# Two layers of cross-attention on one core: feature blocks loaded in quarters, a row load moved in the queue, and three changes of order

## The chip, the core and the metric

The kernel runs on one core of a Trainium2 chip. The core has TensorE (PE in the profile; its weight loads are a row of their own, PEld), VectorE (DVE), ScalarE (ACT), GpSimd (POOL) and SyncE (SP), which here only issues transfers. Sixteen DMA engines carry all transfers. The metric is the device time of one execution in microseconds (us); lower is better.

## The reference

Eight batches of 100 query rows (`x`, 8x100x1024) attend to 1444 context rows of width 512 (`ctx_512`), twice, in fp32. Cut to what is computed:

```python
# layer 0
Q = x @ Wq + bq;  K = ctx @ Wk + bk;  V = ctx @ Wv + bv
w = softmax(Q @ K.T * 1024**-0.5, axis=-1)          # over the 1444 keys
x = x + (w @ V) @ Wo + bo
# layer 1, with its own weights
q = x @ Wq + bq;  k = ctx @ Wk + bk;  v = ctx @ Wv + bv
w = softmax(q @ k.T * 1024**-0.5, axis=1)            # over the 100 queries
y = w @ v + x
out = (y - mean(y)) * rsqrt(var(y) + 1e-6) * gamma + beta
```

## The kernel before

**Algebra.** Keys and values are never made. The kernel multiplies the weights first (`qk` is Wq times Wk transposed, `vo` is Wv times Wo), turns the queries of all batches into `g` (512 rows, 100 columns for each batch), and gets the scores of a batch as context features times `g`. The weighted context `A` (512 x 100) is context rows times softmax weights, and only `A` meets `vo` (layer 0) or Wv (layer 1). So every batch and layer reads the context twice: transposed, as four feature blocks `cT_b_0` to `cT_b_3` of 128 x 1444, and plain, as four row tiles `c_b_0` to `c_b_3` of three 128 x 512 blocks each. Large products go through a seven-product scheme with sums made on VectorE; these are the names `qk_x`, `g_y`, `o_z_x` and so on.

**Stages of the profiled execution.** `qk` of layer 0 to 54 us, `vo` to 100.5, queries of layer 0 to 137, `qk` of layer 1 to 184, then layer 0's scores and weighted rows to 333, its projection to 362, queries of layer 1 to 393, layer 1's scores and weighted rows (with two projections between) to 580, the last batch's projection and normalisation to the end.

**Scores and weighted rows.** `scores_by_keys` (line 941) runs over the four feature blocks k and in each over the twelve key blocks m in the order `KEYS` (8, 11, 9, 10, 0 to 7). `weighted_rows` (902) runs over m = 0 to 11 and four column blocks. From batch 0 on, `alternated` (1317) weaves one step of `A` of batch b with one step of the scores of batch b + 2. TensorE's program order is written out by hand; the order of the other engines is set by a scheduler at build time, except for instructions marked to stay in program order. `vector.in_order` (95) marks VectorE's.

**Loads.** All context loads are issued from SP in program order through `loaded_in_order` (859). In the instruction list each SP transfer waits for one of eight DMA semaphores in turn, which is that of the transfer eight before it, and for the release of its buffer. `load_features` (862) loads each block in two parts, columns 0 to 703 and 704 to 1443. `load_rows` (871) loads a batch's rows in 13 transfers. Buffers go in rotation: row tiles and the first two feature blocks of a batch use the ten buffers of `unit` (74), which the weight products use too; blocks 2 and 3 use the three buffers of `feature_block` (86). So `cT_1_3` takes the buffer of `cT_0_2`, and can be loaded only when the scores of batch 0 have used that. `loaded` (1305) takes blocks from several loads in turn.

**Start of layer 0.** `first_scores` loads four blocks and runs a batch's scores. Lines 1329 to 1332 do batch 0, then batch 1, and `alternated(0)` then loads `c_0` and `cT_2` in turn. SP's order is therefore `cT_0`, `cT_1`, then `c_0_0`, `cT_2_0`, `c_0_1`, `cT_2_1` and so on.

**Softmax.** The key blocks are split in groups `ROWS`: 8 to 10, 0 to 3, 4 to 7, and block 11 (`REST`) by itself. `softmax0` (981) takes maxima, makes the exponents' argument from PSUM and takes the exponent, group by group in that order. `softmax1` (1125) moves the scores out of PSUM with the bias, then for each group finds the maximum over queries and takes exponents, then divides each group (`rtotal`); the order is 8 to 10, 11, 0 to 3, 4 to 7. Both end with `weight_sums` (1159), which adds the blocks on POOL.

**Other places touched.** After the weighted rows of batch 6, the two first parts of `project0` (1041) run: four half products into `o_x` and `o_z`, and an inner seven-product `o_z_*`, each added to `xT` on VectorE by `add_to_queries` (1021). In batch 7, at steps 7, 11 and 15, `queries` (657) is advanced, which issues the sums S1, S2 (`g_s`) and S3 (`qk<-qk`) of layer 1's queries on VectorE; they are not marked in order. In the projection of batches 4 to 6, `project1` (1193) advances batch 7's softmax by 1, 1, 1, 1 and 2 steps in the first five of seven products, and by the rest after the last.

Of the kernel before, what the change touches and what calls it, by code (L numbers as in the profile page):

```python
# [34 lines left out]
S, L = 1444, 512  # L35
EC, LC = E // P, L // P
NQ = 4
MC = 12
# [8 lines left out]
REST = range(11, 12)  # L47
KEYS = (8, 11, 9, 10, *range(8))
LAST = (MC - 1) * P
# [6 lines left out]
def two_layer_cross_attention(ctx: ExitStack, tc: tile.TileContext, a: dict, out: bass.AP):  # L56
# [29 lines left out]
    def feature_block(name):  # L86
        return work.tile([P, S], F32, tag="prob", name=name, bufs=3)
# [16 lines left out]
    vector = Vector()  # L104
# [38 lines left out]
    def run(*parts):  # L143

        parts = list(parts)
        while parts:
            parts = [g for g in parts if next(g, parts) is not parts]
# [714 lines left out]
    def load_features(b):  # L862

        for k in range(LC):
            name = f"cT_{b}_{k}"
            t = feature_block(name) if k >= LC // 2 else unit(name)[:, :S]
            for part in (slice(0, LAST // 2), slice(LAST // 2, S)):
                loaded_in_order(t[:, part], a["ctxT"][b][k * P : (k + 1) * P, part])
            yield t

    def load_rows(b):

        src = a["ctx_512"][b]
        for q in range(NQ):
            t = unit(f"c_{b}_{q}").rearrange("p (c l) -> p c l", c=CQ)
            n = CQ - (q == NQ - 1)
            r0 = q * CQ * P
            for i in range(n):
                loaded_in_order(t[:, i, :], src[r0 + i * P : r0 + (i + 1) * P, :])
            if n < CQ:  # L880
                more = PAD - (S - LAST)
                loaded_in_order(t[: S - LAST, n, :], src[LAST:S, :])
                loaded_in_order(t[S - LAST : PAD, n, :], src[:more, :])
            yield t

    def keys(m):

        return P if m < MC - 1 else S - LAST
# [92 lines left out]
    def softmax0(s, groups, rest):  # L981

        b, w = s["b"], s["w"]
        n = keys(MC - 1)
        last = w[:n, MC - 1, :]
        most = work.tile([P, len(groups), T], F32, tag="most", name=f"most_{b}", bufs=1)
        for g, (ms, r, ps) in enumerate(groups):
            ordered, vector.in_order = vector.in_order, vector.in_order or g == 0
            vector.tensor_reduce(most[:, g, :], ps.rearrange("p c t -> p t c"), AX.X, ALU.max)
            if g == 0:  # L990
                vector.tensor_copy(last, rest[0])
                vector.in_order = ordered
                vector.tensor_tensor(last, rest[1], last, ALU.add)
                vector.tensor_tensor(most[:n, g, :], most[:n, g, :], last, ALU.max)
        groups = [*groups, (REST, n, last.unsqueeze(1))]
        vector.tensor_reduce(top[:, :T], most.rearrange("p g t -> p t g"), AX.X, ALU.max)
        nb = P // QD
        turned = work.tile([QD, nb, nb, QD], F32, tag="turned", name=f"turned_{b}", bufs=1)
        for q in range(nb):
            vector.transpose(turned[:, :, q, :], top[q * QD : (q + 1) * QD, :].rearrange("p (n j) -> p n j", j=QD))  # L1000
        best = small.tile([QD, nb], F32, tag="best", name=f"best_{b}")
        vector.tensor_reduce(best, turned.rearrange("p n q j -> p n (q j)"), AX.X, ALU.max)
        spread = turned[:, :, 0, :]
        vector.tensor_copy(spread, best.unsqueeze(2).to_broadcast([QD, nb, QD]))
        shift = work.tile([P, P], F32, tag="shift", name=f"shift_{b}", bufs=1)
        for q in range(nb):
            vector.transpose(shift[q * QD : (q + 1) * QD, :].rearrange("p (n j) -> p n j", j=QD), spread)
        bias, shift = kb0[:, b * T : (b + 1) * T], shift[:, :T]
        vector.scalar_tensor_tensor(shift, shift, SCALE, bias, ALU.mult, ALU.add)
        vector.tensor_tensor(shift, bias, shift, ALU.subtract)  # L1010
        for ms, r, ps in groups:
            n = len(ms)
            rows = w[:r, ms[0] : ms[0] + n, :]
            vector.scalar_tensor_tensor(
                rows, ps, SCALE, shift[:r].unsqueeze(1).to_broadcast([r, n, T]), ALU.mult, ALU.add
            )
            nc.scalar.activation(rows, rows, AF.Exp)  # L1017
            yield
        weight_sums(s)
# [105 lines left out]
    def softmax1(s, scores, rest):  # L1125

        b, w = s["b"], s["w"]
        groups = []
        for ms, r, ps in [scores[0], (REST, keys(MC - 1), rest[0].unsqueeze(1)), *scores[1:]]:
            n = len(ms)  # L1130
            rows = w[:r, ms[0] : ms[0] + n, :]
            bias = kb1[:r, b * T : (b + 1) * T].unsqueeze(1).to_broadcast([r, n, T])
            ordered, vector.in_order = vector.in_order, vector.in_order or len(groups) < 2
            vector.scalar_tensor_tensor(rows, ps, SCALE, bias, ALU.mult, ALU.add)
            vector.in_order = ordered
            if r < P:
                vector.scalar_tensor_tensor(rows[:, 0, :], rest[1], SCALE, rows[:, 0, :], ALU.mult, ALU.add)
            groups.append((ms, r, rows))
            yield
        made = []  # L1140
        for g, (ms, r, rows) in enumerate(groups):
            negmax, total, rtotal = (
                small.tile([P, GM], F32, tag=n, name=f"{n}_{b}_{g}", bufs=4)[:r, : len(ms)]
                for n in ("negmax1", "total1", "rtotal1")
            )
            vector.tensor_reduce(negmax, rows, AX.X, ALU.max, negate=True)
            for i in range(len(ms)):
                nc.scalar.activation(  # L1148
                    rows[:, i, :], rows[:, i, :], AF.Exp, bias=negmax[:, i : i + 1], accum_out=total[:, i : i + 1]
                )  # L1150
            made.append((rows, total, rtotal))
            yield
        for rows, total, rtotal in made:
            vector.reciprocal(rtotal, total)
            vector.tensor_tensor(rows, rows, rtotal.unsqueeze(2).to_broadcast(list(rows.shape)), ALU.mult)
            yield
        weight_sums(s)
# [144 lines left out]
    batches = [{"b": b} for b in range(B)]  # L1302
    A0 = [wide(f"A0T_{g}") for g in range(2)]

    def loaded(*loads):

        got = [[] for _ in loads]
        for _ in range(NQ):
            for load, to in zip(loads, got):
                to.append(next(load))  # L1310
        return got

    def first_scores(b, layer, softmax):

        return scores_by_keys(batches[b], layer, *loaded(load_features(b)), softmax)

    def alternated(b, layer, softmax, dst, first=0):

        nxt = b + 2 < B
        c, *cT = loaded(load_rows(b), *([load_features(b + 2)] if nxt else []))  # L1320
        A = weighted_rows(batches[b], layer, c, dst)
        ahead = scores_by_keys(batches[b + 2], layer, *cT, softmax) if nxt else iter(())
        run(islice(ahead, first))
        for _ in range(MC * LC):
            next(A)
            next(ahead, None)
            yield

    run(first_scores(0, 0, softmax0))
    block_sums("u1", acc_u, sums[:, :LC, :], late=True)  # L1330
    block_sums("wqbk1", acc_c, sums[:, LC : LC + EC, :], late=True)
    run(first_scores(1, 0, softmax0))
    for b in range(B):
        dst = A0[b // G][:, :, b % G * T : (b % G + 1) * T]
        steps = alternated(b, 0, softmax0, dst, 0 if b else MC)
        if b == B - 2:
            o0 = project0(AS, A0)
            parts = [next(o0), next(o0)]
        if b < B - 1:
            run(steps)  # L1340
        if b == B - 2:
            for part in parts:
                run(part)
        if b == B - 1:
            gT[1], queries1 = queries(1, wqk1, u1)
            for n, _ in enumerate(steps):
                if n in (7, 11, 15):
                    next(queries1)
        for e in range(2 * b, 2 * b + 2) if 2 * b < EC else ():
            add_out_bias(e)  # L1350
        if b == 1:
            got = totals("k1", sums[:, : LC + EC, :], LC + EC)
            u1, wqbk1 = got[:, :LC], got[:, LC:]
            vector.in_order = True
            AS = value_sums(wvo)
            vector.in_order = False
# [5 lines left out]
    steps = queries1  # L1362
# [28 lines left out]
    for bs in SETS:  # L1391
# [10 lines left out]
        if b == B - 2:  # L1402
            first = last_columns(wv1)
# [32 lines left out]
```

## Time and profile before

| What | Value |
|---|---|
| Runs shown | 597.15, 594.76, 597.09 us; median 597.09 |
| The profiled execution's own time | 597.27 us |
| Its span | 595.5 us |
| VectorE, ScalarE, GpSimd busy | 397.5, 134.8, 133.8 us |
| Scores and weighted rows together, share of the chain that ended last | A 21%, s 20% |
| Transfers `c<-in_ctx` of 256 KB | 176, median 6.0 us to landing |
| Transfers `cT<-in_ctxT` of 352 and 370 KB | 64 and 64, median 5.9 and 6.4 us to landing |
| Queue 8, instructions | 59 packets, 0.97 MB |

The span runs from the first to the last of the program's own instructions; the profiled execution's time is 1.77 us longer. Busy shares are averages over stages with different limits, so each step of the prediction is read in its own stretch. In a line of waits the three numbers are the total, the number of waits and the longest; "issue" is a wait for nothing that the profile shows.

### The profile page before, as it was taken

How to read it: one execution, taken by the hardware profiler on the slowest of the kernel's cores; microseconds unless marked ns; L12 is line 12 of the kernel's file. 1: busy time of each engine (PE TensorE's matmuls, PEld its weight loads, DVE VectorE, ACT ScalarE, POOL GpSimd, SP SyncE). 2: the span in 40 equal slices, each digit the busy share in tenths (PEclk: the TensorE clock that was granted, in tenths of full speed). 3: DMA queues.
4: the chain of work that ended last, by engine and by line, in shares of the span. 5: the costliest groups of instructions: out<-in, count | busy, mean ns of one | idle time of the engine just before them, and what ended most of it. 6: DMA issues, size and time to landing. Idle time of an engine off the chain costs nothing.

```text
span 595.5 us, 17451 instructions
## 1 busy us (share of the span) xinstructions
PE 576.7 (97%) x7470; PEld 498.1 (84%) x7470; DVE 397.5 (67%) x936; ACT 134.8 (23%) x349; POOL 133.8 (22%) x206
## 2 busy tenths in 40 slices
PE   9999999999999999999998999999999999999994
PEld 8887457678899899999996766787999999999982
DVE  1997589879676973856648587867433347754795
ACT  1321311423510112222001000203333302153313
POOL 3110110221211222331024001205722202341052
PEclk9999999999999999999999999999999999999998
DMA  8959989943696999999981707709999990699114
GB/s 273 308 107 318 303 217 297 255 86 87 119 277 161 387 378 373 373 342 374 366 290 52 248 0 261 230 21 359 363 372 343 359 341 23 181 324 285 37 30 83
DMA packets 65096, 142.95 MB, mean 240 GB/s; under 512 B 7548, under 2 KB 12924, under 8 KB 65020
## 3 DMA queue, kind: packets, MB, share of 16 engines
q1 hardware_dynamic: 56574, 117.80, 56.5%
q0 software_dynamic: 8048, 23.57, 18.9%
q8 instruction: 59, 0.97, 0.7%
q10 hardware_dynamic: 398, 0.47, 0.3%
q14 instruction: 17, 0.14, 0.1%
HBM read 121.53 MB, written 6.14 MB: 214 GB/s over the span
## 4 chain that ended last, share of the span: by engine, by line
PE 92%; issue 3%; DMA 2%; POOL 2%; DVE 1%; ACT 1%; DVEq 0%; POOLq 0%; SPq 0%
PE A L910 21%; PE s L957 20%; PE qk_x L166 7%; PE g_x L166 5%; PE o_x L166 5%; PE vo_x L166 3%; PE o_y L166 3%; PE g_y L166 3%; PE qk_z L166 2%; PE qk_y L166 2%; DMA cT<-in_ctxT 1%; PE o_w L166 1%; PE o_z L166 1%; PE qk_w L166 1%; PE vo_y L166 1%
## 5 line engine op out<-in xcount | busy, mean ns | idle before, releaser
L910 PE MATMUL A<-w,c 128*64 128x100 f32 (+1 forms) x3072 | 229.2, 249 | 3.9 <-issue 2.4
L910 PEld LDWEIGHTS A<-w,c 128*64 128x64 f32 (+1 forms) x3072 | 200.5, 137 | 6.7 <-issue 6.5
L957 PE MATMUL s<-g1T,cT 128*64 128x100 f32 (+1 forms) x1472 | 114.7, 249 | 1.4 <-issue 1.4
L957 PE MATMUL s<-g0T,cT 128*64 128x100 f32 (+1 forms) x1472 | 112.6, 249 | 3.0 <-issue 1.6
L957 PEld LDWEIGHTS s<-g1T,cT 128*64 128x64 f32 (+1 forms) x1472 | 99.0, 136 | 3.5 <-issue 2.8
L957 PEld LDWEIGHTS s<-g0T,cT 128*64 128x64 f32 (+1 forms) x1472 | 97.5, 136 | 4.9 <-issue 2.6
L1168 POOL TENSOR_TENSOR part<-w 128x500 f32<-128x500 f32 x16 | 23.4, 1462 | 128.7 <-ACT w L1017 61.6
L1148 ACT ACTIVATE w<-w,negmax 128x100 f32<-128x100 f32 x96 | 35.0, 366 | 71.8 <-DVE negmax L99 71.1
L99 DVE SCALAR_TENSOR_TENSOR w<-s,kb 128x400 f32<-128x400 f32 (+2 forms) x32 | 13.9, 462 | 43.6 <-PE s L957 43.4
L1017 ACT ACTIVATE w<-w 128x400 f32<-128x400 f32 (+2 forms) x32 | 12.9, 450 | 122.3 <-DVE w L99 122.3
L99 DVE TENSOR_REDUCE most<-s 128x100 f32<-128x400 f32 (+1 forms) x24 | 12.5, 520 | 39.9 <-PE s L957 39.8
L166 PE MATMUL qk_x<-qk 128*128 128x256 f32 x128 | 31.1, 393 | 0.0
L166 PEld LDWEIGHTS qk_x<-qk 128*128 128x128 f32 x128 | 24.3, 199 | 3.4 <-ACT qk L440 0.2
L1228 DVE SCALAR_TENSOR_TENSOR z<-vectors,r,z 100x512 f32<-100x512 f32 x16 | 11.3, 743 | 13.9 <-PE z L1226 13.9
L969 POOL MEMSET w<- 68x100 f32 x16 | 3.8, 238 | 64.9 <-PE A L910 49.5
L99 DVE TENSOR_TENSOR w<-w,rtotal 128x400 f32<-128x400 f32 (+2 forms) x32 | 17.7, 556 | 0.8
L1148 ACT ACTIVATION_READ_ACCUMULATOR w<-w,negmax 128x1 f32 x96 | 18.0, 187 | 0.0
L1241 ACT ACTIVATE z<-z,rstd 100x1024 f32<-100x1024 f32 x7 | 8.0, 1150 | 43.4 <-POOL rstd L1239 43.4
L99 DVE TENSOR_TENSOR xT<-xT,o_x 128x400 f32<-128x400 f32 (+1 forms) x32 | 16.0, 538 | 1.9 <-PE o_x L166 1.3
L673 ACT ACTIVATE g1T<-g_x,k 128x400 f32<-128x400 f32 x4 | 2.4, 594 | 61.2 <-PE g_x L166 61.1
L578 POOL DMA_DIRECT2D qk_L_xattn_bk<-qk_L_xattn_bk x6 | 5.2, 922 | 45.4 <-ACT qk_L_xattn_bk L583 18.0
L166 PE MATMUL vo_x<-vo 128*128 128x512 f32 x32 | 15.3, 595 | 0.0
(435 smaller groups left out, 1054.1 us busy)
## 6 DMA issues: line engine op xcount, KB each, us to landing
c<-in_ctx SPq DMA_DIRECT2D x176, 256.0 KB, 6.0
cT<-in_ctxT SPq DMA_DIRECT2D x64, 370.0 KB, 6.4
cT<-in_ctxT SPq DMA_DIRECT2D x64, 352.0 KB, 5.9
vo<-in_L_xattn_Wo SPq DMA_DIRECT2D x8, 512.0 KB, 7.4
qk<-in_L_xattn_WqT SPq DMA_DIRECT2D x8, 512.0 KB, 5.5
qk<-in_L_xattn_WqT SPq DMA_DIRECT2D x15, 256.0 KB, 5.1
xT<-in_xT SPq DMA_DIRECT2D x2, 1600.0 KB, 25.1
qk_L_xattn_bk<-qk_L_xattn_bk POOLq DMA_DIRECT2D x6, 512.0 KB, 6.6
```

The costliest lines, as they stand in the source:

```text
L99: ins = getattr(nc.vector, op)(*args, **kw)
L166: nc.tensor.matmul(banks[n // per][:, n % per * width : (n % per + 1) * width], lhs[i][:, n * P : (n + 1) * P], rhs[i], start=(fresh and i ...
L578: nc.gpsimd.dma_start(out=to, in_=t, accum_op=ALU.add)
L673: nc.scalar.activation(dst[g][:, c, :], banks[j][:, :GT], AF.Identity, bias=u[:, c : c + 1])
L910: nc.tensor.matmul(ps[h * HP : (h + 1) * HP, k * T : (k + 1) * T], c[m // CQ][:r, m % CQ, k * P + h * HP : k * P + (h + 1) * HP], w[:r, m, :],
L957: nc.tensor.matmul(to, cT[k][:, o : o + n], q[:, k, t0 : t0 + T], start=(k == 0 and m % GM == 0), stop=(k == LC - 1 or (k == LC - 2 and no ...
L969: nc.gpsimd.memset(s["w"][:PAD, MC - 1, :], 0.0)
L1017: nc.scalar.activation(rows, rows, AF.Exp)
L1148: nc.scalar.activation(rows[:, i, :], rows[:, i, :], AF.Exp, bias=negmax[:, i : i + 1], accum_out=total[:, i : i + 1])
L1168: add(part, w[:, 0:5, :], w[:, 5:10, :], ALU.add)
L1228: nc.vector.scalar_tensor_tensor(z[:, half], bv1[j][:T], s["r"], ps[:T, :], ALU.mult, ALU.add)
L1241: nc.scalar.activation(z, z, AF.Copy, scale=rstd)
```

## The change

Five edits, none of which changes what is computed:

1. Each feature block is loaded in four parts of 361 columns instead of two of 704 and 740.
2. At the start of layer 0 the loads are listed by hand: `cT_0`, three blocks of `cT_1`, all of `c_0`, two blocks of `cT_2`; then scores of batch 0; then `cT_1_3` and `cT_2_2`; then scores of batch 1; then `cT_2_3`. `alternated` takes the loaded tiles of batch 0 as an argument.
3. `softmax0` makes the exponents of blocks 8 to 10 after those of 0 to 3 and 4 to 7.
4. `softmax1` sorts its groups for the second phase: 0 to 3, 4 to 7, 8 to 10, 11.
5. VectorE keeps program order while the first two parts of `project0` run after batch 6, and while `queries` is advanced in batch 7.

```diff
@@ load_features
-            for part in (slice(0, LAST // 2), slice(LAST // 2, S)):
+            for part in (slice(i * S // 4, (i + 1) * S // 4) for i in range(4)):
                 loaded_in_order(t[:, part], a["ctxT"][b][k * P : (k + 1) * P, part])
@@ softmax0
-        groups = [*groups, (REST, n, last.unsqueeze(1))]
+        groups = [*groups[1:], groups[0], (REST, n, last.unsqueeze(1))]
@@ softmax1
+        groups.sort(key=lambda group: group[0][0])
         made = []
@@ alternated
-    def alternated(b, layer, softmax, dst, first=0):
+    def alternated(b, layer, softmax, dst, first=0, got=None):
         nxt = b + 2 < B
-        c, *cT = loaded(load_rows(b), *([load_features(b + 2)] if nxt else []))
+        c, *cT = got or loaded(load_rows(b), *([load_features(b + 2)] if nxt else []))
@@ start of layer 0
-    run(first_scores(0, 0, softmax0))
+    loads = [load_features(b) for b in range(3)]
+    cT = [list(islice(load, n)) for load, n in zip(loads, (LC, LC - 1, 0))]
+    c0 = list(load_rows(0))
+    cT[2] += islice(loads[2], LC // 2)
+    run(scores_by_keys(batches[0], 0, cT[0], softmax0))
+    cT[1] += loads[1]
+    cT[2] += islice(loads[2], 1)
     block_sums("u1", acc_u, sums[:, :LC, :], late=True)
     block_sums("wqbk1", acc_c, sums[:, LC : LC + EC, :], late=True)
-    run(first_scores(1, 0, softmax0))
+    run(scores_by_keys(batches[1], 0, cT[1], softmax0))
+    cT[2] += loads[2]
     for b in range(B):
-        steps = alternated(b, 0, softmax0, dst, 0 if b else MC)
+        steps = alternated(b, 0, softmax0, dst, *((0,) if b else (MC, (c0, cT[2]))))
...
         if b == B - 2:
+            vector.in_order = True
             for part in parts:
                 run(part)
+            vector.in_order = False
...
                 if n in (7, 11, 15):
+                    vector.in_order = True
                     next(queries1)
+                    vector.in_order = False
```

## The prediction

> **What bounds the kernel now.** I read the page's busy line first, then who waited for whom on PE, then the stretch around each long wait.
>
> ```profile
> PE 576.7 (97%) x7470; PEld 498.1 (84%) x7470; DVE 397.5 (67%) x936; ACT 134.8 (23%) x349; POOL 133.8 (22%) x206
> PE s L957 <- issue: 3.0, 6, 0.8
> PE A L910 <- issue: 2.4, 4, 0.7
> PE o_z_x L166 <- DVE xT L99: 1.9, 1, 1.9
> PE A L910 <- DVE rtotal L99: 1.5, 1, 1.5
> PE s L957 <- DMA cT<-in_ctxT: 1.4, 1, 1.4
> ```
>
> PE is the bound: it works through 576.7 of 595.5 us. Its order is the same before and after (the two instruction lists agree row by row), so only PE's waits and the tail behind its last product can change. Three single waits, 1.9, 1.5 and 1.4 us, are what edits 5, 4 and 1+2 can reach; the issue waits, 5.4 us in ten pieces, are not addressed by any edit.
>
> The wait for `cT` is at 203.93 to 205.28. The chain of waits there ends in the second part of `cT_2_1`:
>
> ```profile
> 191.73 0.81 SPq L860 DMA_DIRECT2D cT<-in_ctxT  x2
> 197.40 7.84 DMA cT<-in_ctxT
> ```
>
> The first line is `cT_1_3`, held until `cT_0_2` was used; all of `c_0` and `cT_2` stands behind it in SP's queue, and the last line is the landing that PE waited for.
>
> From then on transfers are the second bound. SP's own waits between 205.4 and 289 us, and two stretches of the table by windows (the last number of a row is GB/s, the one before it the DMA share):
>
> ```profile
> SPq L860 <- DMA cT<-in_ctxT: 19.2, 34, 1.0
> SPq L860 <- DMA c<-in_ctx: 18.2, 51, 0.7
> SPq L860 <- PE s L957: 0.6, 1, 0.6
> ...
> 10.00:14.00 4.00, 4.00 (x20) 3.51 (x20) 0.02 (x1) 1.17 (x2) 0.00 (x0) 1.00 1.02 337
> 205.00:289.00 84.00, 82.01 (x1870) 81.04 (x1871) 50.66 (x142) 14.91 (x28) 22.67 (x44) 1.00 1.04 370
> ```
>
> SP waits 37.4 us for earlier transfers and hardly ever for a buffer: the engines are full at 370 GB/s, and PE is just kept fed. In layer 1 (417 to 486 us) SP waits 11.7 us for `PE s` instead, so there the loads have room.
>
> The other two waits are VectorE's order. First the stretch before PE's wait at 320.6, then the one before its wait at 566.5:
>
> ```profile
> 317.11 1.57 DVE L99 TENSOR_TENSOR g_s<-qk 128x1024 f32<-128x1024 f32 x1
> 318.60 0.56 DVE L939 TENSOR_TENSOR A0T<-A,rrow 128x400 f32<-128x400 f32 x1
> 319.08 1.03 DVE L99 TENSOR_TENSOR xT<-xT,o_x 128x400 f32<-128x400 f32 x2
> 320.04 1.21 DVE L99 TENSOR_TENSOR g_s<-g_s,qk 128x1024 f32<-128x1024 f32 x1
> 321.18 1.04 DVE L99 TENSOR_TENSOR xT<-xT,o_z 128x400 f32<-128x400 f32 x2
> 322.14 0.35 DVE L99 TENSOR_TENSOR xT<-xT,o_z_x 128x200 f32<-128x200 f32 x1
> ...
> 565.99 0.98 DVE L99 TENSOR_TENSOR xT<-xT,o_y 128x300 f32<-128x300 f32 x2 [0.31 <-PE o_y L166]
> 567.09 0.57 DVE L99 TENSOR_TENSOR w<-w,rtotal 128x400 f32<-128x400 f32 x1
> 567.92 0.73 PE L910 MATMUL A<-w,c 128*64 128x100 f32 x12 [1.46 <-DVE rtotal L99]
> 569.26 1.41 DVE L1228 SCALAR_TENSOR_TENSOR z<-vectors,r,z 100x512 f32<-100x512 f32 x2 [0.91 <-PE z L1226]
> ```
>
> Two `g_s` sums stand ahead of the addition that frees `o_z_x`'s bank. And block 0 of batch 7's weights, which `A` needs first, is divided third.
>
> **What the Trainium skill says.** "Perfetto Trace Analysis", section DMA Optimizations, gives both sides of edit 1: splitting lets some work start sooner, but transfers under 2 KB carry marked overhead. A quarter's row is 361 x 4 = 1444 bytes. The trace agrees on the overhead: the 337 GB/s of 10 to 14 us came from 1.35 MB in 1258 packets. "DMA: Bandwidth & Descriptors", section Why small descriptors are slow, has a fixed cost for each packet; this is the form that I use. "Runtime: NRT & Kernel Launch", section Instruction fetch mechanics, says that instructions come by DMA in 16 KiB blocks; the page's queue 8 has 59 packets in 0.97 MB, 16.4 KB each. So the issue waits, which lie in the stretches where the DMA engines are full, may be late instruction blocks; the trace names no cause. [...]
>
> **The change part by part.**
>
> *Edits 1 and 2, the start.* After the change `c_0_0` and `c_0_1` go out as `qk`'s units come free, before 184 us, and `c_0_2`, `c_0_3`, `cT_2_0`, `cT_2_1` when `qk` ends at 184.2: 2.9 MB, 8 us at 370 GB/s, landed by about 193. PE needs `cT_2_1` at 203.9, so the whole 1.35 us goes. `cT_1_3` is now behind these; it still issues near 192, takes about 5 us, and is needed at 199.5 (scores of batch 1 start at 193.5 with 2 us for each block): no new wait. `cT_2_3` waits for `cT_1_2`'s release at 199.5, and `c_1_0` follows at about 200.6, against 208.18 in the profile: loads run 7.5 us ahead of before, after which buffers hold them. Gain 1.35 (bounds 1.0 and 1.6). The early rows share the engines with POOL's accumulating transfers for `wqbk1` (the last was issued at 185.72, needed by VectorE at 201.98), which have ten us to spare.
>
> *Edit 1, the long run.* Sixteen feature transfers a batch for eight, 29 in place of 21 in all. PE gets some ninety waits more; those already met cost nothing, since of all such waits before only the ones shown leave idle time. SP needs 29 x 0.33 to 0.43 us (its transfers' durations by tile, `c` in this stretch and `qk` at the start) = 9.6 to 12.5 us for each batch. PE needs 376 products at 8.24/192 = 42.9 ns, with the row sums' four, 16.3, and about 0.45 of issue waits: 16.75 us. For the rate I fit time per byte = a + c / packet size to two points: 337 GB/s at 1210 bytes (1.35 MB over 1258 less 142 small packets) and 370 at 2413 (31.10 MB over 14591 less 1705). That gives a = 2.438e-3 and c = 0.640; the new mean, 5.98 MB in 3524 packets, is 1697 bytes, so 355 GB/s and 16.85 us a batch, an estimate. It falls behind by 0.1 us a batch over six batches, 0.6 us, against the 7.5 of head start: no cost. Bounds: at 337 GB/s 17.75 us, 6.0 in all, still covered; better than nothing is possible if shorter transfers let instruction blocks through sooner, at most the 2.3 us of issue waits in this stretch, and a loss of 1 us if they delay them.
>
> *Edit 3.* The same operations; only block 8 to 10's bank is freed later, by two times 0.48 us. `s_2` takes that bank again at 201.6 and it is free at 200.5. No cost, no gain: block 0's weights of batch 0 were there anyway.
>
> *Edit 5.* Now reciprocal to 317.1, `A0T` to 317.6, `o_x` additions to 318.6, then wait for PE's `o_z`, which ends at 319.6; its additions to 320.56, `o_z_x` to 320.9. PE goes on at 320.95 instead of 322.54: 1.6 us gained, 0.3 left as wait. The sums follow at 322.7 and end at 326.8; VectorE is idle from 326.0 to 332.8 now, which hides them. Bounds 1.0 and 1.9.
>
> *Edit 4.* Blocks 0 to 3 and 4 to 7 are divided within the room between products (0.57 us each in place of 0.47 and 0.26, beside PE's last products), and blocks 8 to 10 and 11 after `o_y`. PE's `A` starts at 566.5: 1.43 us earlier. But behind it VectorE is full from 569.26 to 583.3, so what counts is when `z` of batch 4 begins: after `o_y`'s additions at 566.97 and one division it is about 568.0, 1.25 us earlier. POOL's `weight_sums` needs 8 to 10 only for its first addition: 567.7 for 568.52. The instruction list has block 11's division after the first half of `z`; POOL needs it last, at 571. The POOL and ScalarE chain of the three normalisations follows VectorE by 0.75 to 1.2. I take 1.2 at the end; bounds 0.3 (POOL's chain alone decides) and 1.5 (PE's).
>
> Sum: 1.35 + 1.6 + 1.2 = 4.15 us; the profiled execution's 597.27 gives 593.1. The median of the runs shown is 0.18 lower, so 593.0.
>
> **Rivals.**
>
> *Part of it comes back.* POOL's chain sets the tail (0.3 in place of 1.2) and the shorter packets add 1 us of issue waits: 597.1 - 1.35 - 1.6 - 0.3 + 1.0 = 594.85. For it: POOL, ScalarE and POOL's transfers alternate on the chain from 568.5 to 584.7. Against: `rstd` there waits for VectorE twice.
>
> *Shorter queues also help instruction blocks.* Eight transfers in flight are 1.64 MB in place of 2.28. If half of the 5.4 us of issue waits goes: 590.3. For it: these waits all lie where the DMA share is about 1. Against: nothing shows that queue 8 stands behind the data queue.
>
> *Slower: the quarters make layer 0 bound by transfers.* Eight in flight may be too few for the latency, 3.4 us for 128 KB at 10 to 14 us, or rows of 1444 bytes at unfavourable addresses cost more than the fit. At 310 GB/s a batch takes 19.3 us, 2.55 more than PE; six batches lose 15.3, less 7.5 of head start is 7.8, and 593.0 + 7.8 = 600.8. It passes the time before at about 320 GB/s (18.7 us, 11.7 - 7.5 = 4.2). For it: PE and the engines are level already. Against: 337 GB/s with still smaller packets and transfers.
>
> **How the numbers follow.** Forecast 0.60, part comes back 0.18, instruction blocks 0.12, slower 0.10. The bound of 0.5% is 3.0 us, about what a measurement of this kernel can tell from no change. Nearly all of the forecast's own range, 591.5 to 594.6, and the third case lie past it; the rest of the forecast and the second within it: faster 0.70, same 0.20, slower 0.10. The range 590.0 to 597.0 leaves out the slower case and a few hundredths on each side.
>
> **What would show it.** PE's list of waits without the three lines, `o_z_x` with about 0.3; SP between 205 and 289 waiting for PE's releases more than for transfers; about 355 GB/s where SP waits for transfers; `A` of batch 7 right behind `o_y`. It is wrong if PE waits for `cT` or `c` anywhere between 220 and 300, if issue waits pass 7 us, or if the span behind the last `A` grows.

## The result, and the profile after

| | before | after |
|---|---|---|
| Median of the runs beside each other | 597.52 us (20 runs) | 593.52 us (20 runs) |
| Ratio, with its 95% interval | | 0.9936 [0.9913, 0.9958] |
| Profiled execution: time, span | 597.27, 595.5 us | 593.5, 591.7 us |

The change makes the kernel 0.64% faster; the forecast was 593.0. The total is as forecast, its parts are not. First the page after: busy times, granted clock in forty slices of 14.8 us, and the two kinds of context loads (number, size of one, median us from issue to landing).

```profile
PE 576.7 (97%) x7470; PEld 499.2 (84%) x7470; DVE 399.0 (67%) x936; ACT 133.1 (22%) x349; POOL 132.0 (22%) x206
PEclk9999999999999889999999999999999999999999
cT<-in_ctxT SPq DMA_DIRECT2D x256, 180.5 KB, 4.7
c<-in_ctx SPq DMA_DIRECT2D x176, 256.0 KB, 5.1
```

PE's busy time is the same to the tenth, though two slices near 200 us show a lower clock. A quarter lands in 4.7 us where the two parts took 5.9 and 6.4; and the row loads, whose size nobody changed, land in 5.1 instead of 6.0. Now the whole list of PE's waits after (total, number, longest):

```profile
PE s L957 <- DMA cT<-in_ctxT: 5.3, 1, 5.3
PE warm L111 <- DVE ones L108: 1.1, 1, 1.1
PE s L957 <- issue: 0.7, 2, 0.5
```

The waits of 1.9, 1.5 and 1.4 us that the prediction wanted gone are gone. So are nearly all of the 5.4 us of issue waits, which it called not addressed. But a new wait of 5.3 us for a feature block has come. PE's timeline shows where (start, duration; in brackets the idle time before and what ended it):

```profile
196.74 3.13 PE L957 MATMUL s<-g0T,cT 128*64 128x100 f32 x67 [0.48 <-issue]
205.20 6.65 PE L957 MATMUL s<-g0T,cT 128*64 128x100 f32 x92 [5.33 <-DMA cT<-in_ctxT]
```

The 92 products at 205.20 are the scores of batch 1 with its fourth block, `cT_1_3`. They also take 6.65 us, where the same 92 took 4.17 in two of the experiments below. The clock says why (PE alone by windows: length, busy, count, granted clock, DMA share, GB/s):

```profile
204.00:208.00 4.00, 2.80 (x34) 0.50 1.05 355
208.00:212.00 4.00, 4.00 (x70) 0.71 1.03 367
```

After the wait PE ran at half clock for some microseconds, 2.5 us lost on top of 5.3. None of it is a wait in the list.

The rest of the comparison is a table of marks, read from PE's timeline in both traces: the start of the row sum (line 929) behind a batch's weighted rows, and the first or last product of a stage.

| Mark | before | after | gained up to here | in this stretch |
|---|---|---|---|---|
| batch 0's row sum | 219.56 | 225.77 | -6.21 | -6.21 |
| batch 5's | 305.11 | 308.45 | -3.34 | +2.87 |
| batch 7's | 332.43 | 333.95 | -1.52 | +1.82 |
| first scores of layer 1 | 393.53 | 395.04 | -1.51 | +0.01 |
| second projection's `o_x` | 485.92 | 483.78 | +2.14 | +3.65 |
| third projection's `o_x` | 552.00 | 549.43 | +2.57 | +0.43 |
| `z` of batch 4 | 568.58 | 564.48 | +4.10 | +1.53 |
| last product | 587.71 | 583.82 | +3.89 | -0.21 |

Read the last column: the start lost 6.2 us, the long run of layer 0 and that of layer 1 gave back 2.9 and 3.65 where no gain was forecast, and the two changes of VectorE's order brought 1.8 and 1.5.

The two long runs gave more than PE's list of waits has there before (2.2 and 2.5 us). A wait in the list begins at the end of a product, and a product lasts 0.25 us while the next starts 0.04 us behind it, so a wait costs about 0.2 us more than the list says (an estimate). And each column is one execution. Layer 0's 2.9 us are not firm: between batch 0's and batch 5's row sums before took 85.6 us and after 82.7, but e8 below, with the loads of before, took 82.9 in its trace. Layer 1's are firmer: from its first scores to the second projection 92.4 us before, 91.7 and 92.2 in the two experiments with halves (e1, e8), 88.7 after.

**The long run.** SP's waits from 205.4 to 285 us after, two stretches by windows (behind PE, PEld, DVE, ACT and POOL stand clock, DMA share and GB/s), and in the last line the first stretch before:

```profile
SPq L860 <- DMA c<-in_ctx: 10.5, 25, 1.1
SPq L860 <- DMA cT<-in_ctxT: 3.9, 11, 0.7
SPq L860 <- PE s L957: 0.3, 1, 0.3
...
215.00:285.00 70.00, 70.00 (x1624) 69.82 (x1621) 44.61 (x126) 12.36 (x25) 17.55 (x32) 1.00 0.97 310
417.00:480.00 63.00, 63.00 (x1468) 62.89 (x1464) 24.99 (x68) 18.96 (x99) 23.91 (x42) 1.00 0.98 326
...
215.00:285.00 70.00, 68.29 (x1562) 67.45 (x1559) 42.05 (x118) 13.26 (x24) 19.67 (x38) 1.00 1.04 370
```

PE is busy for all of the 70 us, before for 68.29 of them. SP still waits for earlier transfers, not for PE: transfers bind here, at 310 GB/s instead of 370, and with a share of 0.97 instead of 1.04. PE is fed because it came 6 us late; e7 below tests this.

**Edit 5** (VectorE, projection after batch 6) and **edit 4** (VectorE and PE, projection of batches 4 to 6) after:

```profile
321.20 1.04 DVE L99 TENSOR_TENSOR xT<-xT,o_x 128x400 f32<-128x400 f32 x2
322.47 1.24 DVE L99 TENSOR_TENSOR xT<-xT,o_z 128x400 f32<-128x400 f32 x2 [0.23 <-PE o_z L166]
323.63 0.35 DVE L99 TENSOR_TENSOR xT<-xT,o_z_x 128x200 f32<-128x200 f32 x1
...
563.41 0.98 DVE L99 TENSOR_TENSOR xT<-xT,o_y 128x300 f32<-128x300 f32 x2 [0.20 <-PE o_y L166]
...
561.68 2.20 PE L166 MATMUL o_y<-A1T,wv_s 128*128 128x150 f32 x16
563.81 0.74 PE L910 MATMUL A<-w,c 128*64 128x100 f32 x12
```

The additions follow each other with no `g_s` sum between them, and `A` starts right behind `o_y` with no wait.

### The profile page after: what moved, and what is told of

It is laid out like the page before. It is cut to its first block, busy times and chain, and to the rows that moved or that the text cites. A ratio compares the mean times of both kernels' runs of the same rounds, so it can differ in the third digit from the quotient of the medians.

```text
span 591.7 us, 17652 instructions
## 1 busy us (share of the span) xinstructions
PE 576.7 (97%) x7470; PEld 499.2 (84%) x7470; DVE 399.0 (67%) x936; ACT 133.1 (22%) x349; POOL 132.0 (22%) x206
## 4 chain that ended last, share of the span: by engine, by line
PE 59%; DMA 19%; issue 5%; SPq 4%; POOL 2%; ACT 1%; DVE 0%; POOLq 0%; DVEq 0%; ACTq 0%
PE s L957 14%; PE A L910 13%; DMA c<-in_ctx 8%; DMA cT<-in_ctxT 6%; PE o_x L166 5%; PE g_x L166 5%; SPq L860 4%; PE qk_x L166 4%; PE o_y L166 3%; PE g_y L166 3%; DMA vo_L_xattn_bv<-vo_L_xattn_bv 2%; DMA g_t<-xT 2%; PE o_w L166 1%; PE o_z L166 1%; PE qk_y L166 1%
## 5 line engine op out<-in xcount | busy, mean ns | idle before, releaser
L910 PEld LDWEIGHTS A<-w,c 128*64 128x64 f32 (+1 forms) x3072 | 198.1, 137 | 1.9 <-issue 1.7
L957 PE MATMUL s<-g0T,cT 128*64 128x100 f32 (+1 forms) x1472 | 114.3, 254 | 5.9 <-DMA cT<-in_ctxT 5.3
L957 PEld LDWEIGHTS s<-g0T,cT 128*64 128x64 f32 (+1 forms) x1472 | 98.9, 140 | 7.3 <-DMA cT<-in_ctxT 6.0
L957 PEld LDWEIGHTS s<-g1T,cT 128*64 128x64 f32 (+1 forms) x1472 | 97.3, 136 | 2.4 <-issue 1.6
## 6 DMA issues: line engine op xcount, KB each, us to landing
cT<-in_ctxT SPq DMA_DIRECT2D x256, 180.5 KB, 4.7
```

What stands on the lines that cost most here:

```text
L910: nc.tensor.matmul(ps[h * HP : (h + 1) * HP, k * T : (k + 1) * T], c[m // CQ][:r, m % CQ, k * P + h * HP : k * P + (h + 1) * HP], w[:r, m, :],
L957: nc.tensor.matmul(to, cT[k][:, o : o + n], q[:, k, t0 : t0 + T], start=(k == 0 and m % GM == 0), stop=(k == LC - 1 or (k == LC - 2 and no ...
```

## The experiments

Eleven kernels ran. e4, e8 and e11 start from the kernel before; the others are the changed kernel with other parts, another order of loads, or both (e10). e5 is to be compared with e1. The diffs are cut to the lines that matter. Each trace is of one execution: e7's is the slowest of its twenty (596.32 us), e8's the fastest of its twelve (591.70). "Before" ran beside them: 595.86 us (e1 to e4), 597.11 (e5 to e8) and 596.34 (e9 to e11).

| Run | Part of a feature block | Median us | Ratio to before, interval | Landing `cT` / `c`, 215 to 285 us | GB/s there | Issue waits |
|---|---|---|---|---|---|---|
| before | halves, 352 and 370 KB | | | 6.0 / 6.2 | 370 | 5.4 |
| after | quarters, 180.5 KB | 593.52 | 0.9936 [0.9913, 0.9958] | 4.8 / 4.8 | 310 | 0.7 |
| e1 | halves | 593.62 | 0.9963 [0.9935, 0.9991] | 6.1 / 5.9 | 359 | 5.2 |
| e2 | halves of 64 rows | 655.83 | 1.0976 [1.0917, 1.1035] | 6.8 / 6.9 | 250 | 6.8 |
| e3 | every other quarter | 648.62 | 1.0845 [1.0776, 1.0914] | 4.9 / 6.5 | 248 | 1.1 |
| e4 | quarters, edit 1 alone | 601.77 | 1.0082 [1.0046, 1.0119] | 5.1 / 5.1 | 317 | none |
| e5 | halves, small ones between | 592.71 | 0.9923 [0.9894, 0.9951] | not in the trace | 333 | 1.4 |
| e6 | thirds, 241 KB | 589.52 | 0.9888 [0.9829, 0.9947] | 5.4 / 5.6 | 341 | 1.2 |
| e7 | quarters, block first | 593.20 | 0.9940 [0.9915, 0.9965] | 5.1 / 4.8 | 316 | 1.4 |
| e8 | halves, edits 3 to 5 alone | 595.14 | 0.9979 [0.9950, 1.0009] | 6.0 / 6.2 | 371 | 3.4 |
| e9 | thirds again | 588.97 | 0.9881 [0.9855, 0.9908] | 5.6 / 5.6 | 350 | 0.6 |
| e10 | thirds, block first | 584.43 | 0.9807 [0.9778, 0.9835] | 5.4 / 5.0 | 347 | 0.7 |
| e11 | thirds, nothing else | 593.89 | 0.9957 [0.9939, 0.9975] | 5.3 / 5.8 | 345 | 0.4 |

Issue waits are sums over PE's list for the whole span; landing is the median from issue to landing.

**e1: the change without the quarters.**

```diff
-            for part in (slice(i * S // 4, (i + 1) * S // 4) for i in range(4)):
+            for part in (slice(0, LAST // 2), slice(LAST // 2, S)):
```

> The changed kernel with edit 1 undone: feature blocks in two parts of 704 and 740 columns again, all other edits kept. Theory (the quarters are behind both findings: they make SP late at the start, and they end the issue waits): PE's wait for cT near 200 us falls from 5.3 to below 1, the transfers between 215 and 285 us run at about 370 GB/s, PE's issue waits come back to about 5 us; the time stays within 1.5 us of the changed kernel's 593.5. Rival (the order of loads of edit 2 makes the wait, whatever the size of the parts): the wait stays at 4 to 6 us, issue waits come back, and the time is 598 to 600.

PE's waits in e1:

```profile
PE s L957 <- issue: 4.5, 11, 0.9
PE warm L111 <- DVE ones L108: 1.1, 1, 1.1
PE A L910 <- issue: 0.7, 3, 0.3
PE s L957 <- DMA cT<-in_ctxT: 0.6, 1, 0.6
```

The new wait shrinks from 5.3 to 0.6 us, and the issue waits are back at 5.2. Both came from edit 1, and inside the whole change they cancel: the two spans are 591.2 and 591.7. SP's timeline tells how the quarters delay `cT_1_3`. First after, then e1 (start, duration of a run of issues, number):

```profile
160.62 21.12 SPq L860 DMA_DIRECT2D cT<-in_ctxT  x20
181.85 9.05 SPq L860 DMA_DIRECT2D c<-in_ctx  x13
192.09 13.56 SPq L860 DMA_DIRECT2D cT<-in_ctxT  x20
```

```profile
159.93 14.31 SPq L860 DMA_DIRECT2D cT<-in_ctxT  x10
174.34 12.93 SPq L860 DMA_DIRECT2D c<-in_ctx  x13
187.68 13.55 SPq L860 DMA_DIRECT2D cT<-in_ctxT  x10
```

The first line is the same five blocks in both: 21.1 us in quarters, 14.3 in halves. While they go out, POOL's accumulating transfers run on another queue. Bytes by queue from 160 to 174 us, after and then e1 (packets, MB, the packets' time as a share of 16 engines; q0 is POOL's, q1 is SP's):

```profile
q0 software_dynamic: 543, 1.97, 78.2%
q1 hardware_dynamic: 931, 1.21, 26.8%
```

```profile
q0 software_dynamic: 496, 1.84, 70.7%
q1 hardware_dynamic: 640, 1.66, 33.6%
```

SP's queue moves 1.21 MB instead of 1.66, in more packets, and POOL's gets more of the engines. "DMA: Bandwidth & Descriptors" of the Trainium skill, section Queues, rings and completion order, says that an engine goes round the queues that have work, one packet at a time. A packet of that page is a group of some 9 to 17 descriptors, while the packets that the profile counts are here the rows of a part, 1444 bytes in a quarter. So the page does not state that short rows lose share; it would follow if a group holds about as many rows of either length, and no run shows the groups. What the traces show is that SP's queue with shorter rows got fewer bytes.

Short rows are not the whole delay. In e5 below the rows are as long as in e1, with fewer bytes in flight. SP's queue moved 1.59 MB from 160 to 174 us, nearly as in e1. Yet the row loads began 18.6 us after the first of the five blocks; in e1 it was 14.4 us and after 21.2.

**e2 and e3: small transfers with long packets.** Both were to part the size of a transfer from that of its packets, the rows of a part. e2 (the first diff) cuts each half again by rows instead of columns; e3 (the second) keeps two transfers, each of every other quarter.

```diff
+                for r in (0, HP):
+                    loaded_in_order(t[r : r + HP, part], a["ctxT"][b][k * P + r : k * P + r + HP, part])
```

```diff
+            src = a["ctxT"][b][k * P : (k + 1) * P, :].rearrange("p (n h c) -> p n h c", n=2, h=2)
+            for h in range(2):
+                loaded_in_order(t.rearrange("p (n h c) -> p n h c", n=2, h=2)[:, :, h, :], src[:, :, h, :])
```

> The changed kernel with each feature block in four transfers of 64 rows by 704 or 740 columns: transfers as small as the quarters (180 and 189 KB), rows in packets as long as before (2816 and 2960 bytes). Theory P (the length of the packets counts): 360 to 375 GB/s between 215 and 285 us, SP as early as with halves at the start, wait for cT below 1 us. Theory F (the bytes in the eight transfers in flight count): 310 to 330 GB/s, wait for cT 4 to 6 us. The issue waits have the same two theories apart: P about 5 us, F below 1.5 us. Where rate goes with P and issue waits with F, the time is near 588.

> The changed kernel with each feature block in two transfers of 370 KB that each take every other quarter: transfers as large as the halves, packets of 1444 bytes. The mirror of the 64-row kernel. Theory P: 310 to 330 GB/s between 215 and 285 us, PE's wait for cT near 200 us of 4 us or more, issue waits below 1.5 us. Theory F: 360 to 375 GB/s, wait below 1 us, issue waits about 5 us.

Both ran far from what was expected. In e2 a packet of 2816 bytes took about 180 ns instead of 127, so a transfer of half the rows is slow by itself: 250 GB/s with the engines full. In e3 SP waited ten times for earlier feature loads between 215 and 285 us, 33.5 us in all and up to 6.1 at once. A reason that fits is that the two transfers of a block have interleaved addresses and the build puts them in order; no run shows it. e3's issue waits (1.1 us) and its wait near 200 us (14.7) came out on the side of theory P, but with loads held back they are no support for it. PE waited 44 and 45 us for features. Neither parts the two causes. One thing can be kept from e2: its transfers are as small as quarters, but land late (6.8 us), and its issue waits stayed (6.8 us in all). So small transfers alone do not end them.

**e4: edit 1 alone, on the kernel before.**

```diff
-            for part in (slice(0, LAST // 2), slice(LAST // 2, S)):
+            for part in (slice(i * S // 4, (i + 1) * S // 4) for i in range(4)):
```

> The kernel before with edit 1 alone: quarters, in the old order of loads. If the quarters hold the long run to about 320 GB/s (18.7 us for a batch where PE needs 16.3), PE has no head start to live on and waits for cT or c for 8 us or more between 200 and 305 us; the time is 603 to 610. If they run at my forecast's 355 GB/s, PE's wait stays at 1.4 to 3 us and the time is 595 to 598.

PE's wait for features in e4, and the long run by windows:

```profile
PE s L957 <- DMA cT<-in_ctxT: 9.1, 13, 1.4
...
215.00:285.00 70.00, 65.71 (x1466) 64.10 (x1468) 41.99 (x118) 10.97 (x21) 14.94 (x28) 1.00 0.97 317
```

There is no issue wait left in this kernel, but PE waits thirteen times for features: 317 GB/s feed a batch (5.98 MB) in 18.9 us, where PE needs 16.3. It is slower than before by 0.8%, a little less than expected. The lower rate that the prediction's slower case feared is real.

**e5: fewer bytes in flight, with long packets.** Halves, and behind each a load of one element into a scratch tile that nothing reads (an addition to what the kernel does). SP lets eight transfers be in flight, and these now fill some of the eight places.

```diff
+                loaded_in_order(scratch[:, n % 16 : n % 16 + 1], a["ctx_512"][0][:1, :1])
```

> The changed kernel with halves again, and after each half a transfer of one element into a scratch tile. Each small one takes one of the eight places in flight, so the eight hold about as few bytes as with quarters, while the packets stay 2816 and 2960 bytes long. If the bytes in flight decide: transfers land in about 5 us in place of 6, and PE's issue waits fall from about 5 us below 1.5; if their length decides: issue waits of 4 us or more. For the rate between 215 and 285 us: bytes in flight 310 to 330 GB/s, packet length 350 or more. Issue waits gone at 350 GB/s would give about 588 us; otherwise 592 to 596.

The long run of e5 by windows, against e1's, which differs only in the small loads:

```profile
215.00:285.00 70.00, 70.00 (x1624) 69.82 (x1622) 42.09 (x118) 12.82 (x24) 20.37 (x38) 1.00 0.97 333
```

```profile
215.00:285.00 70.00, 68.27 (x1554) 67.11 (x1552) 40.95 (x115) 12.81 (x24) 19.00 (x36) 1.00 1.01 359
```

With the same packets, fewer bytes in flight cut the issue waits from 5.2 to 1.4 us and the rate from 359 to 333 GB/s, with the share down to that of the quarters (what the small loads themselves cost is in this). So the issue waits depend on the bytes in flight, and so does part of the loss of rate. The rest, 333 to 310, comes with the short packets: from 215 to 285 us SP's queue moved 23.09 MB in 96.0% of the engines' time in e5 and 21.50 MB in 95.3% after, which is 21.5 and 20.1 bytes per ns of an engine (22.2 in e1). PE waits 2.5 us for `cT_1_3` in e5.

**e7: quarters, with the late block sent first.**

```diff
-    cT[2] += islice(loads[2], LC // 2)
     run(scores_by_keys(batches[0], 0, cT[0], softmax0))
     cT[1] += loads[1]
-    cT[2] += islice(loads[2], 1)
+    cT[2] += islice(loads[2], LC // 2 + 1)
```

> The changed kernel with cT_1_3 in front of cT_2_0 and cT_2_1 in SP's queue. Theory A (the 5.3 us wait, with the half clock that follows it, is plain loss): the wait near 200 us is gone, nothing takes its place, and the time falls by 6 to 8 us to about 586.5. Theory B (at about 318 GB/s layer 0's transfers end when they end, and the wait only let them get ahead): the wait near 200 us falls below 1 us, but PE waits for cT or c between 220 and 305 us instead, 3 us or more in all, and the time is 590 to 595.

```profile
PE s L957 <- DMA cT<-in_ctxT: 6.3, 8, 1.6
...
215.00:285.00 70.00, 67.53 (x1530) 66.31 (x1526) 41.54 (x117) 12.81 (x24) 20.69 (x39) 1.00 0.96 316
```

These are e7's waits for features and its long run. Batch 0's row sum starts at 218.91, 6.9 us earlier than after. But the single wait of 5.3 comes back as eight: six of 3.6 us in all in layer 0, two of 2.7 in layer 1. At the first scores of layer 1 only 0.6 us of the 6.9 are left, and the time is that of after (0.9940 and 0.9936). With quarters, what PE gains at the start it waits for later.

**e6 and e9: thirds.** Rows of 1924 or 1928 bytes, parts of 241 KB; e9 is the same kernel again, with six runs instead of four.

```diff
+            for part in (slice(i * S // 3, (i + 1) * S // 3) for i in range(3)):
```

> The changed kernel with three parts for each block (rows of 1924 or 1928 bytes, 246 KB, 25 transfers a batch in place of 29 or 21). Between halves and quarters on either theory: 335 to 350 GB/s between 215 and 285 us, landing in 5.2 to 5.6 us. If an issue wait is an instruction block that takes longer than PE needs to use one up[...], issue waits are 0 to 2 us. PE's wait for cT near 200 us 2 to 4 us. Time 590 to 593.

> The kernel of e6 a second time, for a firmer interval: e6 had 0.9888 from four runs. If transfers of 241 KB keep the engines fuller than quarters (341 GB/s against 310 between 215 and 285 us) and still land within 5.5 us, the ratio is 0.987 to 0.992, under the changed kernel's 0.9936. If e6 was a lucky set of runs, 0.993 or more, and parts and quarters are alike.

588.97 us in e9, interval 0.9855 to 0.9908, wholly under that of after: thirds beat quarters. They keep 341 to 350 GB/s, and the issue waits stay near 1 us. The wait for `cT_1_3` is 2.9 us in e6 and 3.4 in e9.

**e10: thirds, with the late block sent first** (e7's edit on e9).

> Thirds, with batch 1's fourth feature block sent ahead of batch 2's first two. With thirds the single wait for that block was at most the 2.9 us of all waits for feature blocks. If transfers at about 341 GB/s are what PE is held to between 220 and 300 us, taking the wait away moves PE's work 1 to 2 us earlier and it waits that much more later: no gain over e9 (within 1 us), with waits for feature blocks of about 3 us spread over more places. If 341 GB/s leaves room, the time falls by the wait, 1.5 to 2.5 us under e9.

PE's whole list of waits in e10, and its long run:

```profile
PE warm L111 <- DVE ones L108: 1.1, 1, 1.1
PE A L910 <- issue: 0.7, 2, 0.5
...
215.00:285.00 70.00, 70.00 (x1624) 69.82 (x1620) 42.91 (x119) 12.81 (x24) 19.28 (x38) 1.00 1.01 347
```

584.43 us, 4.5 us under e9: more than either expectation. Two errors of mine. 347 GB/s do leave room: a batch takes 17.2 us, PE 16.3, and the 0.9 us that the loads lose in each batch never uses up their lead, so no wait comes back. And the wait in e9 cost more than its length. PE's timeline there and in e6 (first e9, then e6):

```profile
202.98 5.83 PE L957 MATMUL s<-g0T,cT 128*64 128x100 f32 x92 [3.36 <-DMA cT<-in_ctxT]
```

```profile
202.41 4.17 PE L957 MATMUL s<-g0T,cT 128*64 128x100 f32 x92 [2.87 <-DMA cT<-in_ctxT]
```

After 3.36 us of waiting the 92 products took 5.83 us, after 2.87 us only 4.17, the undisturbed time. The clock from 204 to 208 us was 0.57 in e9 and 1.00 in e6. So the wait in e9's trace cost 3.36 + 1.66 = 5.0 us, about the difference to e10. e10 is the fastest kernel of all, 1.9% under before.

The length of a wait does not decide alone whether the clock falls. In e5 a wait of 2.47 us, shorter than e6's, was followed by half clock, and in e11 so was one of 1.92 us, the wait for `xT` that before has as well. First e5, then e11 (a line of the timeline, and PE alone by windows):

```profile
202.39 5.83 PE L962 MATMUL s<-g0T,cT 128*64 128x100 f32 x92 [2.47 <-DMA cT<-in_ctxT]
204.00:206.00 2.00, 2.00 (x29) 0.50 0.97 315
```

```profile
320.98 0.60 PE L166 MATMUL o_z_x<-o_t,o_t 128*128 128x200 f32 x2 [1.92 <-DVE xT L99]
322.00:324.00 2.00, 2.00 (x13) 0.50 0.00 0
```

Before waited 1.93 us at the same place, and its clock from 322 to 324 us was 1.00. The half clock does not grow with the wait either: from 202 to 208 us e5's windows of 2 us have 0.78, 0.50 and 0.87, which makes 3.4 us at half clock, and e9 and e11, with waits of 3.36 and 1.92 us, come to 3.4 us as well. After, with 5.33 us, it is 6.8. What decides whether a wait brings it is not shown.

**e8 and e11: one part of the change alone**, on the kernel before: e8 has edits 3 to 5, e11 has thirds and nothing else.

> The kernel before with edits 3, 4 and 5 alone, loads as before. By my working the waits of 1.9 us for xT and 1.5 us for rtotal go and the end is 1.6 + 1.2 = 2.8 us earlier: ratio 0.994 to 0.9965 to the kernel before. The wait for cT of about 1.4 us and about 5 us of issue waits stay. If the gains of the orders came only together with the loads, the ratio is 0.998 or more.

> The kernel before with three parts instead of two and nothing else: no head start from edit 2, and edits 3 to 5 left out. Theory: thirds land within 5.5 us, so the issue waits fall from 5.4 us to under 2, and about 341 GB/s (17.5 us a batch against PE's 16.4) takes 1 us a batch back over six batches without a head start; the three single waits of 1.9, 1.5 and 1.4 us stay. So 594 to 598 us, ratio 0.995 to 1.001, against 1.0082 for quarters alone. Rival, that only transfers' sizes as such count and thirds lie midway between halves and quarters: ratio 1.003 to 1.005.

e8's interval holds most of its expectation, and no change as well. Its trace, that of its fastest execution, lacks the waits for `xT` and `rtotal`, and its marks gain 1.9 us between batch 5's and batch 7's row sums and 1.5 from the third projection's `o_x` to `z`, like after. That the orders are worth some 3 us is read from traces; the times do not show it by themselves. e11 is 0.43% faster than before with no other edit, where quarters alone are 0.8% slower: the size of the parts, and with it the length of their rows, decides, not splitting as such.

## Why the prediction was right in its number and wrong in its parts

- **Edits 4 and 5** went as worked out. Predicted 1.2 and 1.6 us; the marks show 1.5 and 1.8. The wait of about 0.3 us that was to stay at `o_z_x` is not in PE's list. One sign of being wrong came true, in small: the span behind the last `A` grew, from 15.4 to 15.7 us.
- **Edits 1 and 2, the start: wrong.** The step that failed is "it still issues near 192, takes about 5 us, and is needed at 199.5: no new wait". `cT_1_3` went out from 198.7 on and landed at 205.2. The step had given SP's 2.9 MB "8 us at 370 GB/s", the rate of a later stretch, and asked of POOL's transfers only whether they had time to spare, not what they take from SP's. From 160 to 182 us the engines carried 250 GB/s in all after and 291 in e1. Predicted +1.35 us, measured -6.2.
- **The size of that wait.** A wait can cost the clock too. "TensorE: Matmul & The Clock Gate" of the Trainium skill, section HAM oscillation — how this bites in real kernels, gives the rule: no idle gap of TensorE over about 3.4 us. The traces agree with it only in part: half clock after 5.33 and 3.36 us, none after 2.87 us, but half clock also after 2.47 us (e5) and 1.92 us (e11), well under the page's figure. Here the measurement decides: the length is no safe bound. The prediction had no wait at the start and priced the waits that it had at their length.
- **Edit 1, the long run: the rate was mis-sized.** The fit by packet size gave 355 GB/s; it was 310 in after, 317 in e4. The fit took both of its points with the engines full; it had no term for engines that run short of work, and e5 shows that fewer bytes in flight cost 26 GB/s. The bound of 2 KB that the prediction names is one for transfers, and a quarter is 180.5 KB; to apply it to rows of 1444 bytes was the prediction's own step. It also took "337 GB/s" as the lower bound, from a stretch with other transfers. "7.5 us of head start: no cost" was then right only by the accident of the first error: PE was held up at the start, and had its wait in advance. e7, which takes that wait away, gets most of it back in pieces. Two signs of the forecast failed here: 355 GB/s, and SP waiting for PE's releases more than for transfers (0.3 us against 14.4).
- **Issue waits: wrong.** "Not addressed by any edit" was the error that paid. The prediction had allowed at most 2.3 us for layer 0 as a bound and a rival with half of 5.4 us at a chance of 0.12. PE's list falls from 5.4 to 0.7 us. The marks give +3.65 us in layer 1, and +2.87 between batch 0's and batch 5's row sums, most of which e8's trace has with the old loads.
- **The sum.** Of 4.15 us predicted, edits 4 and 5 brought 3.35. The rest is -6.2 at the start against +2.87, +3.65 and +0.43 in the long runs, nearly nothing. A forecast that had missed only one of these two would have been off by 6 us or more. That the number came out was luck.

**Why issue waits go.** e5 shows that they shrink with fewer bytes in flight, with long packets too. e2 has parts as small as quarters and keeps them, but its loads land late. Both fit one measure, the time that a load takes to land. In the table the waits are 3.4 to 6.8 us where both kinds of load land in about 6 us or more (before, e1, e2, e8), and at most 1.4 where they land in 4.8 to 5.8 (after, e4, e6, e7, e9 to e11; e3, with 4.9 and 6.5, has 1.1). These are single traces: before and e8 have the same loads and differ by 2.0 us.

A cause that fits is that instruction blocks queue behind the loads. "Runtime: NRT & Kernel Launch" of the Trainium skill, section Instruction fetch mechanics, has blocks of 256 instructions, here 128 products with their weight loads, 5.5 us at 42.9 ns each (an estimate from the page's figure). A block that takes longer than that to come would be late. But the page calls the cost of going from block to block mostly hidden, and no view shows a block being waited for. So this stays argued; what the runs show is the dependence on what is in flight.

What stays open: how much of the slow start comes from short rows and how much from fewer bytes in flight; what decides whether a wait brings half clock; how much of e8's gain is in its time.

## What to carry to other kernels

The size in which loads are cut sets three things at once: the rate, the share against other queues, and how long everything else, instructions perhaps among it, stands behind the data in flight. Neither end is best; try sizes between (here 241 KB beat 180 and 360 KB), then look at who waits at the joints between stages. A load order has to be priced with the rate of its own stretch, with the other queues that run there, and a wait of TensorE with the clock that it may lose: behind waits of 2.5 to 5.3 us the products here lost another 1.7 to 2.5 us in three traces of four.

## What the runs showed of the hardware

- Behind waits of TensorE of 5.33, 3.36 and 2.47 us the clock fell to about half, and 92 products took 6.65, 5.83 and 5.83 us instead of 4.17; behind one of 2.87 us there was no loss. The same wait of 1.9 us was followed by half clock in one trace (e11) and by full clock in another (before).
- Half clock lasted 3.4 us behind waits of 1.92, 2.47 and 3.36 us alike, and 6.8 us behind one of 5.33.
- From 215 to 285 us an engine moved 22.2 bytes per ns with half-block parts (e1), 21.5 with half-block parts and small loads between (e5), 20.1 with quarters (after).
- Feature loads of 64 rows moved at 250 GB/s with the engines full, a packet of 2816 bytes taking about 180 ns instead of 127 in loads of 128 rows.
- The same half-block loads moved 359 GB/s with eight data loads in flight, and 333 when loads of four bytes took some of the places.
